# A grouped 3 x 3 convolution on one core: 5 of 8 images combined instead of 3 of 5, and one measurement pass moved ahead of a copy in the ramp

## The chip, the cores and the metric

The kernel runs on one core of a Trainium2 chip. Five engines work side by side: PE multiplies matrices into PSUM banks, DVE (VectorE), ACT (ScalarE) and POOL (GpSimd) do the work per element, SP issues most DMAs. The metric is the device time in microseconds (us); smaller is better. A profiled execution gives a span, from its first to its last instruction, and is timed itself as well.

## The reference

160 images of 128 channels and 32 x 32 pixels are each normalised in 32 groups of 4 channels. Then comes a 3 x 3 convolution with padding 1, 128 channels in and 128 out. Image number 32n + b of the kernel is image b of set n: each of five sets has weights of its own, which are first rounded down to two levels. The input is added to the result.

```python
beta, alpha = max(U), min(U)
s1 = (beta - alpha) / 3.0
v1 = s1 * floor(U / s1)
s2 = s1 / 5.0
v2 = s2 * floor((U - v1) / s2)
w = (v1 + v2).reshape(OUT_CH * N, IN_CH, 3, 3)
xb = gn(x).reshape(B // N, N * C, H, W)          # gn: 32 groups, eps 1e-5
act = conv(xb, w, padding=1, feature_group_count=N)
out = x + act.reshape(B, C, H, W)
```

## The kernel before

**Precision.** A normalised image is split into a high part in fp16 (`hi`, or `vh`) and the fp16 rest (`lo` and its combinations `rows`, or `vl`). Both are multiplied by the integer weights and summed in PSUM.

**Two kinds of images.** Every image has two PSUM banks, `even` and `odd`. Before the main products the even bank gets sums that serve both (`begin` with quarter 2 of the operand, `complete` with quarter 3). Then ACT copies the even bank to `half` (`leave`, L907), and DVE makes the odd bank out of twice `half` minus the even bank (`odd_from_even`, L914). So `complete` comes after the copy `half` and after `begin`, `odd_from_even` after `complete`, and `main(i, 0)`, which writes the even bank again, after `odd_from_even`.

- An *uncombined* image is split as it is. The low part is combined by rows on DVE (`low_part`, `combinations`: L747, L760, L768, L769), and the high part goes through all taps. `begin` and `complete` take 3 matmuls each, the two `main` 12 each: 30.
- A *combined* image is first combined by columns in f32: POOL does the outer columns and a difference (L674, L704), DVE the rest (`combine`: L686, L693). ACT scales it to `vh` (L734), DVE makes `vl` (L740). All four blocks take 6 matmuls: 24.

`combined(i)` decides, by the number alone: none below 7, the odd ones below 30 (`FIFTHS`), i % 5 in {0, 2, 4} below 130 (`THIRDS`), three of four after that.

**Statistics.** ACT reads each image twice, for its sum (L241) and for its squares (L248), unless the image is one of eight in `BY_VECTOR`, which DVE measures. Groups of 8 images from 24 on (of 2 and 4 before) share the small steps: PE averages over channels, DVE, ACT (`ve`), POOL (`rstd`) and DVE make the scale. For an uncombined image `z` is normalised by POOL (L710); for the first image of a group, and the first seven of all, by ACT (L636), which for these also needs DVE's `shift`. A measurement runs up to 16 images ahead.

**Order.** The schedule is written by hand: each engine runs its instructions in the order in which the program names them. The loop over i calls `conv(i, ...)` for PE and hangs the other engines' work for later images around it: in iteration i, from 14 on, DVE makes the low part of image i + 3, ACT the high part of i + 4, POOL and DVE the combination of i + 5. ACT's order in an iteration is: `half`, the first pass of a measurement, the copies of the two banks of image i - 1 to `sum` (L942), the high part, the second pass, now and then a step of the weights (L134, L564).

From `TWO_AHEAD` = 28 on (`steady`), PE does `complete` of i + 1, `begin` of i + 2 and then the two `main` of i, and ACT makes the copy of i + 2 after the first passes. In the ramp before that, PE does `begin` of i + 1, `main(i, 0)`, `complete` of i + 1, `main(i, 1)`, and the copy of i + 1 is named in `conv`, ahead of the passes.

Weights of the next set are quantised in small steps between the images (`Later`), mostly on DVE, with two of each column's steps on ACT. The store of the input (SP) and the adding store of `sum` (POOL, L963) write the result. Loads run 18 images ahead as far as the 11 buffers allow.

Of the kernel before, what the change touches and what calls it, by code (L numbers as in the profile page):

```python
# [36 lines left out]
class Later:  # L37
# [25 lines left out]
    def finish(self):  # L63
        run(self.steps)
# [110 lines left out]
def last_of(steps, last=None):  # L175
    for last in steps:
        pass
    return last


def run(steps):

    while True:
        try:
            next(steps)
        except StopIteration as end:
            return end.value
# [134 lines left out]
def general_path(tc, keep, steps, x, u, out):  # L322
# [8 lines left out]
    with tc.If(far > 0), ExitStack() as ctx:  # L331
# [9 lines left out]
        for n in range(N_SETS):  # L341
            un = one.tile([P, C, TAPS], F32, tag="u", name=f"g_u{n}")
            nc.sync.dma_start(un, uv[n])
            wn = one.tile([P, C, TAPS], F32, tag="w", name=f"g_w{n}")
            k1, k2 = run(steps.quantise(one, un, f"g{n}", F32))
            nc.vector.tensor_scalar_mul(wn, k1, steps.s1)
            nc.vector.scalar_tensor_tensor(wn, k2, steps.s2, wn, ALU.mult, ALU.add)
# [38 lines left out]
class Main:  # L386
# [23 lines left out]

    STAT_LEAD = 15
    FURTHER = 11
    TWO_AHEAD = 28
    LOAD_LEAD = 18
    CHUNKS = 11
    STEADY = 7
# [174 lines left out]
    def keep_sums(self, n, col):  # L591
        wt = self.wts[n, col]
        run(self.both_sums(
            self.nc.gpsimd, wt[:, self.SUM], wt[:, self.DIFF], *(wt[:, k] for k in range(ROW))
        ))
# [51 lines left out]
    def combined(self, i):  # L647

        if i < self.STEADY or i >= self.imgs:
            return False  # L650

        if i < self.FIFTHS:
            return i % 2 == 1
        return i % 5 % 2 == 0 if i < self.THIRDS else i % 4 != 2

    def by_scalar_too(self, i):

# [201 lines left out]
    def steady(self, i):  # L859

        return i >= self.TWO_AHEAD

    def conv(self, i, on_the_way):


        ahead = range(i + 1, self.imgs)[:1]
        if self.steady(i) and self.steady(i - 1):
            for k in ahead:
                self.complete(k)
            for k in range(i + 2, self.imgs)[:1]:  # L870
                self.begin(k)
            self.main(i, 0, lambda: on_the_way(self.COLS[1]))
            self.main(i, 1, lambda: on_the_way(self.COLS[2]))
        elif i == self.FIRST:
            self.main(i, 0)
            self.begin(i + 1)
            on_the_way(self.COLS[1])
            self.main(i, 1)
            on_the_way(self.COLS[2])
            self.leave(i + 1)  # L880
            self.complete(i + 1)
        else:
            self.begin(i + 1)
            self.main(i, 0, lambda: on_the_way(self.COLS[1]))
            self.leave(i + 1)
            self.complete(i + 1)
            if self.steady(i):
                self.begin(i + 2)
            self.main(i, 1, lambda: on_the_way(self.COLS[2]))
        del self.v[i]  # L890
# [102 lines left out]
    def run(self):  # L993
# [54 lines left out]
        def measure(stage, *images):  # L1048
            for i in images:
                self.measure(i, (stage,))  # L1050
# [71 lines left out]
        ready, middle, scaled, measured, loaded = [], [], [], self.EARLY, 6  # L1122
        due = [(c, c) for c in range(1, loaded)]
        later, turned = Later(), []
        for i in range(self.imgs):
# [3 lines left out]
            def on_the_way(col):  # L1129
                if col == self.COLS[1]:  # L1130
                    for st in ready:
                        st.means(self.pg)
                    for *column, parts in self.columns:
                        self.turn_column(*column, parts)
                        turned.append(column)
                    self.columns.clear()
                if col == self.COLS[2]:
                    for st in middle:
                        st.variances()

            if i < self.FIRST:
                if i == self.FIRST - 1:
                    self.begin(self.FIRST)
                    self.leave(self.FIRST)

                j = (i - 1) % self.FIRST
                self.direct_hi(j, self.COLS[2])
                self.direct_lo(j, self.COLS[2])
                if i == self.FIRST - 1:
                    self.complete(self.FIRST)  # L1150
                if i == 0:
                    self.stats[2].variances()
                    self.stats[2].deviation()
                    self.stats[2].power()
                    self.stats[2].scales()
                    run(self.sums_across(0, nc.gpsimd))
                for col in self.COLS:
                    on_the_way(col)
            else:
                j = i - 1  # L1160
                self.conv(i, on_the_way)
            ahead = i + min(10 + i // 3, self.STAT_LEAD + 1)
            to_measure = range(measured, min(self.imgs, ahead))
            measured += len(to_measure)
            if i == 2:
                self.load_set(1)
            if b == self.per_set - 8 and n + 2 < N_SETS:
# [5 lines left out]
                        36 / (self.per_set - 6 - b),  # L1173
                    )
            later.next_image()
            by_scalar = [k for k in to_measure if not self.by_vector(k)]
            by_vector = [k for k in to_measure if self.by_vector(k)]

            if i < self.FIRST:

                if i == 0:
                    measure(0, 8, 9, 10)
                if i == 1:
                    self.normalise(4)
                    self.high_part(4)
                if i == 2:
                    self.normalise(5)
                    measure(1, 9)
                    self.high_part(5)
                    self.odd_from_even(3)  # L1190
                    self.low_part(4)
                    run(self.combinations(4))
                    measure(0, 11)
                self.residual(j)
            else:

                last = None
                for k in self.step_of(i, 2):
                    if self.combined(k):
                        last = last_of(self.low_combined(k), last)  # L1200
                    else:
                        self.low_part(k)
                        later.take(1)
                        last = last_of(self.combinations(k), last)
                last = later.take(1, last)
                if last:
                    before = self.last_but_one(last)
                    for st in scaled:
                        self.after(st.power(), before)
                    for k in self.step_of(i, 4):  # L1210
                        self.beside_pairs(k, before)
                if i > self.FIRST and self.by_hand(j):
                    self.residual(j)
                for k in by_scalar:
                    self.measure(k, (0,))
                if self.steady(i) and i + 2 < self.imgs:
                    self.leave(i + 2)
                if i > self.FIRST and not self.by_hand(j):
                    self.residual(j)
                    self.accumulate(j)  # L1220
                for st in ready:
                    if not st.late:
                        st.deviations()
                for k in self.step_of(i, 3):
                    if self.combined(k):
                        self.high_combined(k)
                        continue
                    if self.by_scalar_too(k):
                        self.normalise(k)
                    self.high_part(k)  # L1230
                for k in by_scalar:
                    self.measure(k, (1,))
# [95 lines left out]
```

## Time and profile before

| | |
|---|---|
| device time, median of 3 runs | 972.56 us |
| lowest and highest | 971.38 and 973.38 us |
| the profiled execution's own time | 971.98 us |
| its span | 970.2 us, granted clock 0.993 |
| PE busy | 928.3 us, 96% |
| ACT busy | 863.3 us, 89% |
| DVE busy | 858.9 us, 89% |
| POOL busy | 446.0 us, 46% |
| DMA | 254.23 MB, mean 262 GB/s |

The profiled execution lies 0.58 us below the median of the runs, and 1.8 us of its time are outside the span. Busy shares are means over the whole span. The stages are: start and weights to about 40 us, the ramp with one image ahead to about 220 us, the steady stretch to about 800 us, then 30 images three of four of which are combined, and the end. In the ramp and in the steady stretch different things can set the pace, so the busy times are read by stage.

### The profile page before, as it was taken

Reading aid. Unit: us, or ns where it says so; the run is one execution under the profiler, and the core shown is the slowest. Engines: PE = TensorE matmul, PEld = TensorE weight load, DVE = VectorE, ACT = ScalarE, POOL = GpSimd, SP = SyncE. Lnnn points to the kernel's source line nnn. Section 1 sums busy time; section 2 is a strip of 40 time slices with the busy share of each in tenths; the row PEclk is TensorE's granted clock in tenths of the full one; section 3 lists DMA queues with packets and bytes.
Section 4 is the critical chain, followed back from the end, with each engine's and each line's share of the span. In section 5 each row is a group of like instructions: output and inputs, shape, how many; then the busy total and the mean of one; then the engine's idle time right before and its main releaser. Section 6 shows DMA issues by size and latency. Waiting matters only on the chain.

```text
span 970.2 us, 12948 instructions
## 1 busy us (share of the span) xinstructions
PE 928.3 (96%) x4432; PEld 434.6 (45%) x4432; DVE 858.9 (89%) x1125; ACT 863.3 (89%) x1320; POOL 446.0 (46%) x481
## 2 busy tenths in 40 slices
PE   2899979999999999999999999999999999999996
PEld 1444434444444444444444444444444444444442
DVE  7988878888899899998999899898989988889973
ACT  5779879998999999999999999999999999997660
POOL 4354433544453443454445444545444455454640
PEclk9999989999999999999999999999999999999998
DMA  9079999999999999999999999999999999756554
GB/s 353 29 270 351 329 353 330 328 326 329 321 314 317 259 283 294 276 284 269 290 252 308 286 282 284 289 277 297 263 274 266 290 280 258 162 90 102 95 93 128
DMA packets 67450, 254.23 MB, mean 262 GB/s; under 512 B 5296, under 2 KB 5296, under 8 KB 67376
## 3 DMA queue, kind: packets, MB, share of 16 engines
q1 hardware_dynamic: 45344, 173.09, 47.8%
q0 software_dynamic: 22032, 80.23, 44.1%
q8 instruction: 37, 0.61, 0.2%
q14 instruction: 37, 0.30, 0.1%
HBM read 89.19 MB, written 164.10 MB: 261 GB/s over the span
## 4 chain that ended last, share of the span: by engine, by line
PE 79%; ACT 10%; DVE 5%; issue 3%; DMA 2%; POOL 1%; SPq 0%; DVEq 0%; ACTq 0%; POOLq 0%
PE even L839 43%; PE odd L839 14%; PE even L784 11%; PE odd L784 11%; ACT junk L248 2%; ACT vh L734 2%; ACT sum L942 2%; ACT junk L241 2%; DMA u<-in_L_conv_U_dram 2%; ACT z L636 1%; ACT half L907 1%; ACT hi L644 1%; DVE ext L508 1%; DVE ext L509 1%; DVE lo L747 1%
## 5 line engine op out<-in xcount | busy, mean ns | idle before, releaser
L839 PEld LDWEIGHTS <-wt 128*128 128x128 f16 x1884 | 184.3, 99 | 211.2 <-issue 4.4
L740 DVE SCALAR_TENSOR_TENSOR vl<-v,rstd,vh 128x2048 f16<-128x2048 f32 x94 | 235.2, 2502 | 48.6 <-ACT vh L734 48.4
L839 PE MATMUL even<-vh,across 128*128 128x512 f16 x564 | 211.3, 375 | 3.5 <-ACT half L907 3.5
L839 PE MATMUL even<-vl,across 128*128 128x512 f16 x564 | 211.3, 375 | 1.7 <-DVE vl L740 1.7
L734 ACT ACTIVATE vh<-v,rstd 128x2048 f16<-128x2048 f32 x94 | 190.2, 2024 | 0.0
L784 PEld LDWEIGHTS <-wt 128*128 128x128 f16 x1242 | 121.7, 100 | 144.2 <-issue 6.6
L248 ACT ACTIVATE junk<-xt,mv 128x1024 uint8<-128x1024 f32 x152 | 176.4, 1160 | 0.3
L839 PE MATMUL even<-rows,wt 128*128 128x512 f16 x567 | 174.2, 381 | 2.5 <-ACT half L907 2.4
L963 POOL DMA_DIRECT2D out_dram<-sum x153 | 135.2, 884 | 89.7 <-ACT sum L942 74.5
L241 ACT ACTIVATE junk<-xt 128x1024 uint8<-128x1024 f32 x152 | 161.2, 1060 | 12.7 <-DMA xt<-in_x_dram 9.8
L839 PEld LDWEIGHTS <-across 128*128 128x128 f16 x1128 | 110.4, 98 | 135.5 <-issue 7.5
L784 PE MATMUL even<-hi,wt 128*128 128x496 f16 (+3 forms) x594 | 162.9, 379 | 4.8 <-DVE odd L914 3.8
L710 POOL TENSOR_SCALAR z<-xt,ngm,rstd 128x1024 f32<-128x1024 f32 x49 | 91.8, 1873 | 152.1 <-DVE rows L769 50.5
L784 PE MATMUL odd<-hi,wt 128*128 128x496 f16 (+3 forms) x594 | 161.0, 375 | 0.0
L686 DVE TENSOR_TENSOR v<-xt 128x960 f32<-128x960 f32 x94 | 155.8, 1658 | 0.5 <-POOL v L674 0.5
L907 ACT COPY half<-even 128x512 f32<-128x512 f32 x157 | 90.6, 577 | 60.1 <-PE even L839 57.1
L674 POOL TENSOR_SCALAR v<-xt,ngm 128x64 f32<-128x64 f32 x94 | 59.0, 628 | 172.8 <-DVE vl L740 74.8
L914 DVE SCALAR_TENSOR_TENSOR odd<-half,even 128x512 f32<-128x512 f32 x157 | 107.8, 687 | 17.3 <-PE even L839 13.8
L839 PE MATMUL even<-vh,wt 128*128 128x496 f16 (+1 forms) x282 | 105.6, 375 | 0.0
L839 PE MATMUL even<-vl,wt 128*128 128x496 f16 (+1 forms) x282 | 105.6, 375 | 0.0
L839 PE MATMUL odd<-vl,wt 128*128 128x496 f16 (+1 forms) x282 | 105.6, 374 | 0.0
L839 PE MATMUL odd<-vh,wt 128*128 128x496 f16 (+1 forms) x282 | 105.6, 374 | 0.0
(148 smaller groups left out, 1131.1 us busy)
## 6 DMA issues: line engine op xcount, KB each, us to landing
xt<-in_x_dram SPq DMA_DIRECT2D x78, 1024.0 KB, 9.6
out_dram<-sum POOLq DMA_DIRECT2D x153, 512.0 KB, 8.8
out_dram<-xt SPq DMA_DIRECT2D x76, 1024.0 KB, 14.2
out_dram<-xt SPq DMA_DIRECT2D x7, 512.0 KB, 6.1
u<-in_L_conv_U_dram SPq DMA_DIRECT2D x4, 576.0 KB, 14.7
xt<-in_x_dram SPq DMA_DIRECT2D x4, 512.0 KB, 9.8
range<-in_L_conv_U_dram SPq DMA_DIRECT2D x3, 576.0 KB, 8.0
u<-in_L_conv_U_dram SPq DMA_DIRECT2D x2, 288.0 KB, 3.0
```

The lines of the kernel that those rows point to most:

```text
L241: self.nc.scalar.activation(junk, image, ACTF.Copy, scale=-1.0 / image.shape[1], accum_out=self.mv[:, j, 0:1],)
L248: self.nc.scalar.activation(junk, image, ACTF.Square, bias=self.mv[:, j, 0:1], accum_out=self.mv[:, j, 1:2],)
L674: return self.nc.gpsimd.tensor_scalar(self.view(self.v[i], 0, (512 + W // 2 - 1, 2), (W // 2, H)), self.view(self.image(i), 1, (W - 3, 2), ...
L686: nc.vector.tensor_tensor(self.view(v, 1, (511, 2), (half, H), (1, half - 1)), self.view(x, 1, (1, 2), (W, H), (2, half - 1)), self.view(x ...
L710: ins = nc.gpsimd.tensor_scalar(z, self.image(i), st.ngm[:, j], st.rstd[:, j], ALU.add, ALU.mult)
L734: self.nc.scalar.mul(vh, self.v[i], st.rstd[:, j])
L740: yield self.nc.vector.scalar_tensor_tensor(vl, self.v[i], st.rstd[:, j], self.hi[i], ALU.mult, ALU.subtract)
L784: nc.tensor.matmul(target[a][:, first:end, c0:c1], self.wts[n, col][:, k, :], tile[:, s0 : s0 + 2 * (end - first) - 1 : 2, c0 + dw : c1 + dw],
L839: self.nc.tensor.matmul(out, weights, moving, start=start and j == 0, stop=False, skip_group_check=True)
L907: self.nc.scalar.copy(half, self.eo[i][0])
L914: self.nc.vector.scalar_tensor_tensor(odd, self.half.pop(i), 2.0, even, ALU.mult, ALU.subtract)
L963: added = self.nc.gpsimd.dma_start(self.ov[n, :, b], self.sum.pop(i), accum_op=ALU.add)
```

## The change

Three edits. `combined` takes, between 30 and 130, the images with i * 5 % 8 < 5, that is i % 8 in {0, 2, 4, 5, 7}. `TWO_AHEAD` becomes 20. And for i from 4 to 19 the first pass of the first image that ACT measures in this iteration is named inside `conv`, between `main(i, 0)` and `leave(i + 1)`; to have it there, the list of images to measure is made before `conv` instead of after it. Where an iteration measures a second image on ACT, its first pass stays behind the copy.

```diff
-    TWO_AHEAD = 28
+    TWO_AHEAD = 20
...
         if i < self.FIFTHS:
             return i % 2 == 1
-        return i % 5 % 2 == 0 if i < self.THIRDS else i % 4 != 2
+        return i * 5 % 8 < 5 if i < self.THIRDS else i % 4 != 2
...
-    def conv(self, i, on_the_way):
+    def conv(self, i, on_the_way, between):
...
             self.begin(i + 1)
             self.main(i, 0, lambda: on_the_way(self.COLS[1]))
+            between()
             self.leave(i + 1)
             self.complete(i + 1)
             if self.steady(i):
...
+            ahead = i + min(10 + i // 3, self.STAT_LEAD + 1)
+            to_measure = range(measured, min(self.imgs, ahead))
+            measured += len(to_measure)
+            by_scalar = [k for k in to_measure if not self.by_vector(k)]
+            by_vector = [k for k in to_measure if self.by_vector(k)]
+            first_of = by_scalar[:1] if self.FIRST < i < self.TWO_AHEAD else []
...
                 j = i - 1
-                self.conv(i, on_the_way)
-            ahead = i + min(10 + i // 3, self.STAT_LEAD + 1)
-            to_measure = range(measured, min(self.imgs, ahead))
-            measured += len(to_measure)
+                self.conv(i, on_the_way, lambda: measure(0, *first_of))
...
-            by_scalar = [k for k in to_measure if not self.by_vector(k)]
-            by_vector = [k for k in to_measure if self.by_vector(k)]
-
...
-                for k in by_scalar:
+                for k in by_scalar[len(first_of):]:
                     self.measure(k, (0,))
```

## The prediction

> **What bounds the kernel now.** I read the page first (busy shares, the row of slices), then the busy time by stage, then the timelines of PE, ACT and DVE in the stages where PE is not full.
>
> ```profile
> span 970.2 us, 12948 instructions
> PE 928.3 (96%) x4432; PEld 434.6 (45%) x4432; DVE 858.9 (89%) x1125; ACT 863.3 (89%) x1320; POOL 446.0 (46%) x481
> ...
> PE   2899979999999999999999999999999999999996
> ...
> 100.00:160.00 60.00, 52.40 (x242) 24.07 (x241) 51.91 (x83) 51.21 (x80) 19.37 (x22) 0.94 1.04 343
> ...
> 137.00:142.00 5.00, 5.00 (x13) 1.87 (x13) 2.81 (x2) 2.19 (x3) 3.52 (x5) 0.52 1.03 419
> ...
> 160.00:240.00 80.00, 79.31 (x384) 37.33 (x383) 68.73 (x97) 73.73 (x118) 40.24 (x44) 1.00 1.04 327
> 240.00:520.00 280.00, 280.00 (x1345) 131.31 (x1343) 258.46 (x321) 272.49 (x422) 129.60 (x132) 1.00 1.02 288
> 520.00:800.00 280.00, 280.00 (x1349) 131.56 (x1347) 255.94 (x329) 271.98 (x417) 135.04 (x135) 1.00 1.00 282
> 800.00:880.00 80.00, 78.35 (x373) 36.41 (x372) 69.77 (x70) 76.15 (x116) 40.40 (x40) 1.00 0.77 164
> ```
>
> The stage rows give stretch, length, busy us of PE, PEld, DVE, ACT, POOL, granted clock, DMA share, GB/s. From 240 to 800 (images 33 to 129) PE has no idle time at all; ACT is 97% busy, DVE 92%. There, work taken off PE shortens the run as long as ACT (7.5 and 8.0 us idle in the two rows) keeps up. The ramp loses PE time at 100 to 160, and the clock drops there.
>
> ```profile
> 117.55 0.38 PE L839 MATMUL even<-vh,across 128*128 128x512 f16 x1
> ...
> 118.82 0.80 PE L784 MATMUL even<-hi,wt 128*128 128x512 f16 x3
> ...
> 122.95 0.80 PE L784 MATMUL odd<-hi,wt 128*128 128x512 f16 x3
> ...
> 125.50 0.81 PE L839 MATMUL even<-rows,wt 128*128 128x512 f16 x3
> 126.15 0.38 PE L839 MATMUL even<-vh,wt 128*128 128x512 f16 x1
> ...
> 137.00 1.41 PE L784 MATMUL even<-hi,wt 128*128 128x512 f16 x3 [2.79 <-DVE odd L914]
> ...
> 171.74 0.81 PE L839 MATMUL even<-rows,wt 128*128 128x512 f16 x3 [0.69 <-ACT half L907]
> ```
>
> ```profile
> 90.29 0.81 PE L839 MATMUL even<-rows,wt 128*128 128x512 f16 x3 [0.45 <-ACT half L907]
> ```
>
> ```profile
> 89.68 0.56 ACT L907 COPY half<-even 128x512 f32<-128x512 f32 x1
> ...
> 100.83 0.59 ACT L907 COPY half<-even 128x512 f32<-128x512 f32 x1 [2.54 <-PE even L839]
> ...
> 820.57 0.57 ACT L907 COPY half<-even 128x512 f32<-128x512 f32 x1
> ...
> 826.27 0.57 ACT L907 COPY half<-even 128x512 f32<-128x512 f32 x1
> ...
> 831.57 0.59 ACT L907 COPY half<-even 128x512 f32<-128x512 f32 x1 [0.45 <-PE even L839]
> ```
>
> ```profile
> 128.37 0.16 DVE L296 TENSOR_SCALAR twice<-small 128x4 f32<-128x4 f32 x1 [1.26 <-ACT wt L564]
> ```
>
> Columns: start, length, engine, line, operation; in brackets the idle time before it and what ended it. Images are counted by the program's order. PE waits for `half` (the copy of the even bank) at 90.29 and 171.74, ACT waits for PE at 100.83, DVE waits at 128.37 for ACT's `wt`, PE at 137.00 for DVE's `odd`.
>
> **The change, part by part.**
>
> (1) *5 of 8 instead of 3 of 5.* Counting 30 to 129: before 60 combined images, after 62 (60 in 32..127, then 31 and 128). A combined image is four blocks of 6 matmuls, each 1.27 us (117.55 to 118.82): 5.08. An uncombined one is two blocks of 3 at 0.65 (125.50 to 126.15) and two of 12 at 2.55 (122.95 to 125.50): 6.40. Two images at 1.32: **-2.6 us of PE**, where PE is the bound.
>
> The Trainium skill ("TensorE: Matmul & The Clock Gate", "Wait — 56ns, not 53.3ns?") gives a warm matmul N / 2.4 GHz plus about 2.5 ns. By that the blocks of 12 are 2.50 and of 3 0.63, an uncombined image 6.26, and two images would bring 2.4. The row says that matmuls with 16 x 31 strided columns don't get the shorter time; I take 2.6.
>
> On the other engines: ACT, two `vh` (2.02) for two `hi` (1.06), +1.9. All group starts from 32 on become combined, where before five (48, 56, 88, 96, 128) were not and had their `z` on ACT: -5 x 1.25 = -6.3. ACT -4.4 in all. DVE: (2.50+1.66+0.74) for (1.22+0.69+0.42+0.42) twice, +4.3, less five `shift`: hidden in DVE's 8% idle (21 us per 280). POOL +9.0 (two more of 0.63+1.08, three more `z` of 1.87) at 47% busy. DMAs keep number and order on both queues. If this cover were gone, the +4.3 of DVE alone would eat the gain.
>
> (2) *Evenness of the pattern.* Between two `half` copies ACT takes 5.70 if the image normalised there is combined (820.57 to 826.27 in its timeline), 4.8 if not (826.27 to 831.57 less 0.45 to 0.54 of wait: idle 0.45, and the pass before it ends in a short read of its sum). PE's stretch is complete(i+1), begin(i+2), main(i). The new order C N C N C C N C has four combined of five. Lead of the copy at place 6: at most what one combined main leaves, 2.54-0.6 = 1.9 (trace 1.75 to 1.9). The next stretch is 0.65+1.27+2.54 = 4.46 against ACT's 5.70: lead at place 7 is **0.65**. The old order never goes below 1.6 by the same working, but its `z` took 1.25 off: around images 47 to 49 and 87 to 89 its leads are 0.05 to 0.2, and PE still shows no gap. The new order has no `z`. Places 129, 130 (two uncombined) bring the lead to about 0.1 once. Quantising steps (0.6 to 0.9) can fall before place 7; I allow **+0.3** in all, with 0 and +3 as ends (12 times 0.25).
>
> (3) *The first pass ahead of the copy, i = 4 to 19.* In 13 iterations (copies 6 to 8, 10 to 19) a pass of 1.06 stands before `half`. Behind it on ACT wait that copy, then both `sum` copies; for the copy wait PE's complete and DVE's `odd`. Where ACT was waiting for PE (copies 10 and 16: 2.54, 6.92) the pass is free; elsewhere the copy is 1.06 later. The pass reads a chunk issued 20 us or more before (65.16 for the pass at 101.31; median landing 9.6): no new DMA wait.
> Followed through: copy 6 had a lead of 0.44, PE loses 0.6; copy 8 had none, PE is now 1.06 late in all (90.29 becomes 91.35). From then on PE is late itself, and copies up to 14 find it so: the delays don't add. At copy 10 ACT spends 1.06 of its wait on the pass, but starts 1.06 later; `wt` at 127.86 therefore stands where it stood. DVE's chain from 128.37 hangs on it, and PE's restart at 137.00 on that chain's `odd`. **So the 1.06 is swallowed there: 0.** Were `wt` 1.06 earlier, -1.06; were PE's lateness kept, +1.06: these are the ends.
> From 146.55 ACT is a pass ahead, and copy 20 has no pass before it (image 34 is measured by DVE): it comes 1.06 earlier, and the stall of 0.69 goes: **-0.7**. Next in line is DVE's `odd` of 20, 1.7 ahead of its use.
>
> The clock: PE's gaps around 130 are 1.28, 1.70 and 2.79, none over 2.8, yet the granted clock is 0.52 over 137 to 142: 13 matmuls in 5.0 us, about 2.3 lost. The same page ("What's actually happening") puts the half rate after an idle window of about 3.4 us; by it gaps like these cost nothing, and mine after (1.3, 0.6, 2.8) would be free too: 2.3 less. The trace says that a bunch of shorter gaps is enough, and I take the loss as kept: 0, ends -2.3 and +2.3.
>
> (4) *Two ahead from 20 instead of 28.* No instruction added; `begin` of images 22 to 29 comes one image earlier. So far their low parts end 6.3 to 9.5 us ahead of it; one image takes off 5.7, so 0.6 to 3.8 stay, and ACT, free of its waits, brings them earlier. PE has no gap at 172 to 240, so the four ACT waits it removes (0.44, 0.74, 1.20, 0.28) bring nothing: 0. If the leads were gone, eight waits of up to 1 us.
>
> Sum against the profiled execution: 971.98 (span 970.2) -2.6 +0.3 -0.7 = 969.0. The median of the runs is 0.58 above that execution: **969.5**.
>
> **Rivals.**
> *ACT becomes the bound in the new runs.* For: 97% busy, lead 0.65. If each of 12 cycles costs 0.25, 3.0 goes back in place of 0.3: 972.2, no change. Against: ACT's sum falls by 4.4.
> *Slower: the late copies starve PE in the ramp.* If each delay is paid in full beyond its lead (copies 6: 0.62, 8: 1.01, 11: 1.01, 12: 0.78, 14: 1.01, 17: 0.86, 18: 1.01, 19: 0.65), 7.0: 972.56-2.6-0.7+7.0 = 976.3. It decides once the ramp loses over 3.3 us (2.6 + 0.7), for slower by over 0.2% once it loses 5.2. Against: the lateness is shared, and 137.00 hangs on DVE.
> *The ramp gains.* `wt` earlier and the clock kept: -1 to -3 more, 967.5.
> *The change hardly does what it says*: 60 to 62 images is little, and if the 2.6 were offset nothing but the 0.7 would be left: 971.9; it goes with no change.
>
> **How the numbers follow.** This kernel's measurement tells about 0.2% (1.9 us) from no change: faster means below 970.6, slower above 974.5. Sum as worked out: 0.59. Ramp gains: 0.12. ACT bound or nothing left: 0.14. Ramp starved: 0.15. Faster 0.71, same 0.14, slower 0.15. The likeliest case alone spans 968.3 to 970.5. For 8 in 10 the range takes the ramp gain down to 966.8 and the no-change cases up to 972.8, leaving out the starved ramp and the far end of the gains.
>
> **What would show it.** Right: PE busy without gap from about 172 to 800, that stretch 2.6 shorter; 12 fewer matmuls; 12 `z` on ACT instead of 17; at 90 a gap of about 1 before complete(8); no gap at complete(20); the restart of main(14) again at about 137. Wrong: PE gaps ended by `half` once per eight images after 240; PE still late by 1 us or more at 146; gaps in 172 to 240 ended by `vl` or `rows`.

## The result, and the profile after

| | before | after |
|---|---|---|
| device time, median of 5 runs each, side by side | 971.38 us | 967.40 us |
| lowest and highest | 970.93 and 973.38 | 966.99 and 968.49 |
| ratio, with its 95% interval | | 0.9954 (0.9940 to 0.9968) |
| the profiled execution's own time and span | 971.98, 970.2 us | 968.49, 966.7 us |

The changed kernel is 4.0 us faster in the medians (0.41%), and 0.46% by the ratio, which would be 4.5 us. 969.5 was predicted, from a median of 972.56: a difference of 3.1 us. The profiled execution of the changed kernel is the slowest of its five.

First the page of the changed kernel, then its busy time by stage (stretch, length, busy us of PE, PEld, DVE, ACT, POOL, granted clock, DMA share, GB/s):

```profile
span 966.7 us, 12926 instructions
...
PE 926.6 (96%) x4420; PEld 433.7 (45%) x4420; DVE 866.8 (90%) x1118; ACT 860.8 (89%) x1315; POOL 447.3 (46%) x488
...
PE   2899989999999999999999999999999999999996
```

```profile
40.00:60.00 20.00, 19.16 (x90) 8.89 (x89) 15.68 (x35) 14.77 (x24) 10.26 (x20) 0.91 0.25 88
...
100.00:160.00 60.00, 53.39 (x244) 24.38 (x242) 51.81 (x84) 50.74 (x80) 19.19 (x22) 0.94 1.04 344
160.00:240.00 80.00, 80.00 (x388) 37.66 (x387) 70.15 (x98) 75.53 (x118) 43.42 (x45) 1.00 1.05 324
240.00:520.00 280.00, 280.00 (x1346) 131.48 (x1345) 262.62 (x322) 271.35 (x420) 131.05 (x135) 1.00 1.01 290
520.00:800.00 280.00, 280.00 (x1349) 131.65 (x1348) 261.80 (x324) 270.90 (x418) 136.33 (x138) 1.00 1.01 284
800.00:880.00 80.00, 78.33 (x373) 36.39 (x372) 71.67 (x71) 76.06 (x115) 35.77 (x41) 1.00 0.76 156
```

4420 matmuls instead of 4432. From 160 to 800 PE is full: the idle 0.7 us of the row 160 to 240 is gone, and the two long rows are full as before, although DVE has 4.2 and 5.9 us more to do there (258.46 and 255.94 before). ACT has 1.1 us less in each.

The PE timeline of the ramp, at the places that the prediction followed (start, length, engine, line, operation; in brackets the idle time before it and what ended it):

```profile
91.48 0.81 PE L839 MATMUL even<-rows,wt 128*128 128x512 f16 x3 [0.75 <-ACT half L908]
...
130.09 0.81 PE L839 MATMUL even<-rows,wt 128*128 128x512 f16 x3 [1.33 <-ACT half L908]
...
133.19 0.38 PE L839 MATMUL even<-vl,across 128*128 128x512 f16 x1 [0.66 <-DVE vl L740]
...
137.19 1.41 PE L784 MATMUL even<-hi,wt 128*128 128x512 f16 x3 [2.80 <-DVE odd L915]
...
171.61 0.81 PE L839 MATMUL even<-rows,wt 128*128 128x512 f16 x3
```

complete(8) comes at 91.48 instead of 90.29, the restart of main(14, 0) at 137.19 instead of 137.00, and complete(20) has no gap in front of it. What the restart hangs on stands nearly where it stood, in the timelines of ACT and DVE:

```profile
128.06 0.47 ACT L564 ACTIVATE wt<-small 128x384 f16<-128x384 f32 x1
128.44 1.04 ACT L241 ACTIVATE junk<-xt 128x1024 uint8<-128x1024 f32 x1
129.38 0.19 ACT L241 ACTIVATION_READ_ACCUMULATOR junk<-xt 128x1 f32 x1
129.47 0.57 ACT L908 COPY half<-even 128x512 f32<-128x512 f32 x1
```

```profile
128.56 0.16 DVE L296 TENSOR_SCALAR twice<-small 128x4 f32<-128x4 f32 x1 [1.14 <-ACT wt L564]
```

The second line of ACT is the moved pass, now ahead of the copy; `wt` is at 128.06. In the timeline of the kernel before it is

```profile
127.86 0.47 ACT L564 ACTIVATE wt<-small 128x384 f16<-128x384 f32 x1
```

**A ledger by image.** In each trace take the end of the last matmul into the odd bank of an image, less the same end in the trace before. A minus means earlier than before, in us. The columns that matter: at image 0 nothing of the change has acted; from 18 to 31 lies complete(20); from 31 to 129 lies the steady stretch with the new pattern.

| end of odd of image | 0 | 6 | 10 | 14 | 18 | 31 | 129 | 159 | 31 to 129 |
|---|---|---|---|---|---|---|---|---|---|
| after | +0.88 | +0.89 | +1.19 | +0.60 | +0.73 | -0.14 | -3.00 | -2.97 | -2.86 |
| pattern alone | +0.02 | +0.02 | -0.23 | -0.91 | -0.91 | -0.93 | -3.78 | -3.73 | -2.85 |
| two ahead alone | +1.05 | +1.05 | +0.81 | +1.09 | +1.09 | +1.08 | +1.06 | +1.06 | -0.02 |
| pass alone | -0.02 | +0.81 | +1.25 | -0.42 | -0.28 | -1.13 | -1.18 | -1.14 | -0.05 |
| all, two passes only | +0.14 | +0.14 | -1.04 | -0.89 | -0.89 | -1.34 | -4.20 | -4.17 | -2.86 |

Of the 3.5 us between the two spans 2.97 stand at the last matmul; the rest lies behind it (8.3 us from there to the end before, 7.3 to 7.9 in the five kernels of the table), where nothing was changed, and why it differs is not known.

### The profile page after: what moved, and what is told of

Read it like the earlier page. It is cut to its first block, busy times and chain, and to the rows that moved or that the text cites. A ratio compares the mean times of both kernels' runs of the same rounds, so it can differ in the third digit from the quotient of the medians.

```text
span 966.7 us, 12926 instructions
## 1 busy us (share of the span) xinstructions
PE 926.6 (96%) x4420; PEld 433.7 (45%) x4420; DVE 866.8 (90%) x1118; ACT 860.8 (89%) x1315; POOL 447.3 (46%) x488
## 4 chain that ended last, share of the span: by engine, by line
PE 84%; ACT 8%; DVE 4%; issue 2%; POOL 1%; DMA 0%; DVEq 0%; ACTq 0%
PE even L839 45%; PE odd L839 15%; PE even L784 12%; PE odd L784 11%; ACT vh L734 2%; ACT junk L248 2%; ACT sum L943 1%; ACT junk L241 1%; ACT z L636 1%; DVE ext L508 1%; DVE ext L509 1%; ACT half L908 0%; ACT hi L644 0%; DVE lo L747 0%; DVE tt L144 0%
## 5 line engine op out<-in xcount | busy, mean ns | idle before, releaser
L740 DVE SCALAR_TENSOR_TENSOR vl<-v,rstd,vh 128x2048 f16<-128x2048 f32 x96 | 239.2, 2491 | 37.2 <-ACT vh L734 37.1
L839 PE MATMUL even<-vh,across 128*128 128x496 f16 (+1 forms) x576 | 216.1, 375 | 3.5 <-ACT half L908 3.5
L839 PE MATMUL even<-vl,across 128*128 128x496 f16 (+1 forms) x576 | 215.8, 375 | 0.7 <-DVE vl L740 0.7
L734 ACT ACTIVATE vh<-v,rstd 128x2048 f16<-128x2048 f32 x96 | 194.1, 2022 | 0.0
L839 PE MATMUL even<-rows,wt 128*128 128x512 f16 x549 | 168.6, 381 | 2.2 <-ACT half L908 2.1
L686 DVE TENSOR_TENSOR v<-xt 128x960 f32<-128x960 f32 x96 | 163.3, 1702 | 0.0
L784 PE MATMUL even<-hi,wt 128*128 128x496 f16 (+3 forms) x576 | 158.5, 380 | 4.6 <-DVE odd L915 3.8
L710 POOL TENSOR_SCALAR z<-xt,ngm,rstd 128x1024 f32<-128x1024 f32 x52 | 86.3, 1660 | 160.7 <-DVE vl L740 75.3
L784 PE MATMUL odd<-hi,wt 128*128 128x496 f16 (+3 forms) x576 | 156.8, 376 | 0.0
L674 POOL TENSOR_SCALAR v<-xt,ngm 128x64 f32<-128x64 f32 x96 | 66.3, 691 | 160.8 <-DVE vl L740 86.3
```

What stands on the lines that cost most here:

```text
L674: return self.nc.gpsimd.tensor_scalar(self.view(self.v[i], 0, (512 + W // 2 - 1, 2), (W // 2, H)), self.view(self.image(i), 1, (W - 3, 2), ...
L686: nc.vector.tensor_tensor(self.view(v, 1, (511, 2), (half, H), (1, half - 1)), self.view(x, 1, (1, 2), (W, H), (2, half - 1)), self.view(x ...
L710: ins = nc.gpsimd.tensor_scalar(z, self.image(i), st.ngm[:, j], st.rstd[:, j], ALU.add, ALU.mult)
L734: self.nc.scalar.mul(vh, self.v[i], st.rstd[:, j])
L740: yield self.nc.vector.scalar_tensor_tensor(vl, self.v[i], st.rstd[:, j], self.hi[i], ALU.mult, ALU.subtract)
L784: nc.tensor.matmul(target[a][:, first:end, c0:c1], self.wts[n, col][:, k, :], tile[:, s0 : s0 + 2 * (end - first) - 1 : 2, c0 + dw : c1 + dw],
```

## The experiments

Each ran beside the kernel before on the same chip; ratios are to that.

**Pattern alone.**

```diff
-        return i % 5 % 2 == 0 if i < self.THIRDS else i % 4 != 2
+        return i * 5 % 8 < 5 if i < self.THIRDS else i % 4 != 2
```

> Only the 5 of 8 pattern is taken over; the order in the ramp and the 28 stay. Theory (PE is the bound from 240 to 800 and pays by the matmul): 12 matmuls fewer give 2.6 us, and the five group starts without z on ACT give some tenths more where the copy of the even bank had no lead left; so 2.6 to 3.0 us less than before, PE without idle time from 240 to 800, and the ramp as before (PE waits of 1.28, 1.70, 2.79 at 128 to 137, 0.69 at copy 20). Rival (ACT is the bound, and the gain comes from the five z that left it): up to 6 us less.

968.73 us, ratio 0.9968 (0.9956 to 0.9980), 3.1 us less. In the ledger 2.85 come between images 31 and 129. The 0.91 up to image 14 is not the pattern's, which starts at 30: in that execution the clock was at half rate for 3.4 us at 134 to 143 instead of 6.8 (granted clock 0.81 there, 0.62 before; the reading stands under the pass alone).

**Two ahead from 20, alone.**

```diff
-    TWO_AHEAD = 28
+    TWO_AHEAD = 20
```

> Only the start of working two ahead is moved from 28 to 20; pattern and pass order stay. Theory: PE has no idle time in 172 to 240 but for 0.69 before copy 20, so nothing to win: within 0.7 us of before, and ACT's four waits of 0.28 to 1.20 there shrink. Rival (the low parts of images 22 to 29 come too late one image earlier): PE waits ended by vl or rows, 1 to 4 us slower.

972.22 us, ratio 1.0000 (0.9991 to 1.0008). The ledger is flat from 14 to 159; the 1.05 stands there from image 0 on (the clock at 40 to 44, last section). This edit is worth nothing by itself, though ACT's waits for PE at the copies fall from 6.0 to 4.1 us between 172 and 240.

**The pass alone**, in i = 4 to 19, with the old pattern and TWO_AHEAD at 28:

```diff
+            first_of = by_scalar[:1] if self.FIRST < i < 20 else []
...
-                self.conv(i, on_the_way)
+                self.conv(i, on_the_way, lambda: measure(0, *first_of))
```

> Only the pass is moved ahead of the copy, for i from 4 to 19; pattern and 28 stay. Theory: PE is up to 1 us late after copy 8, that is swallowed where main of image 14 waits for DVE's odd (at about 137 as before), and the 0.69 before copy 20 goes: 0.5 to 0.8 us less than before. Rival (each late copy is paid in full): 7 us more than before.

970.18 us (20 runs), ratio 0.9983 (0.9976 to 0.9990): 1.7 us less, more than the 0.5 to 0.8 expected. The PE timeline shows the steps as worked out:

```profile
77.59 0.81 PE L839 MATMUL even<-rows,wt 128*128 128x512 f16 x3 [0.66 <-ACT half L908]
...
91.54 0.81 PE L839 MATMUL even<-rows,wt 128*128 128x512 f16 x3 [0.89 <-ACT half L908]
...
137.23 0.80 PE L784 MATMUL even<-hi,wt 128*128 128x512 f16 x3 [2.80 <-DVE odd L915]
...
170.60 0.81 PE L839 MATMUL even<-rows,wt 128*128 128x512 f16 x3
```

Copy 6 costs 0.66, copy 8 brings the lateness to 1.25, the restart at 137.23 swallows all but 0.23, and complete(20) has no gap (-0.85 from 18 to 31). What had not been expected is the drop from +1.25 to -0.42 across image 14. It is the clock, in the busy time of two stretches of this kernel:

```profile
134.00:143.00 9.00, 6.20 (x23) 2.43 (x21) 6.05 (x9) 6.09 (x12) 5.24 (x6) 0.81 1.04 409
137.00:142.00 5.00, 4.77 (x15) 1.89 (x15) 3.05 (x3) 3.34 (x5) 3.52 (x5) 0.66 1.03 422
```

and of the changed kernel:

```profile
134.00:143.00 9.00, 6.20 (x17) 2.26 (x16) 6.01 (x9) 6.06 (x12) 5.27 (x6) 0.62 1.04 411
137.00:142.00 5.00, 4.80 (x12) 1.77 (x12) 3.01 (x3) 3.34 (x5) 3.52 (x5) 0.50 1.02 419
```

PE is busy for the same 6.20 of 9 us, but 23 matmuls against 17: 0.81 over 9 us is 3.4 us at half rate, 0.62 is 6.8.

**A pass ahead in two iterations only.** The changed kernel with

```diff
-            first_of = by_scalar[:1] if self.FIRST < i < self.TWO_AHEAD else []
+            first_of = by_scalar[:1] if i in (9, 15) else []
```

so that no copy of a short lead is delayed, and the pass still goes into ACT's waits at copies 10 and 16.

> The changed kernel, but with the pass ahead of the copy only at i = 9 and 15, where ACT waits for PE anyway (2.54 and 6.92 us). Theory (DVE's chain before main of image 14 hangs on ACT's wt, and the passes at i = 5 to 7 made PE late, so that wt gained nothing): copy 8 is in time as before, wt comes 1.06 us earlier, and so main of image 14: 1 us less than the changed kernel, 4.5 us less than before. Rival (that restart hangs on DVE's own queue, or on the clock, not on wt): the same as the changed kernel within 0.3 us.

966.74 us, ratio 0.9946 (0.9932 to 0.9959). Its timelines of ACT, DVE and PE:

```profile
126.79 0.47 ACT L564 ACTIVATE wt<-small 128x384 f16<-128x384 f32 x1
```

```profile
127.29 0.16 DVE L296 TENSOR_SCALAR twice<-small 128x4 f32<-128x4 f32 x1 [1.21 <-ACT wt L564]
```

```profile
135.93 1.41 PE L784 MATMUL even<-hi,wt 128*128 128x512 f16 x3 [2.80 <-DVE odd L915]
```

`wt` is 1.07 us earlier than before the change, and so are `twice` (1.08) and the restart (1.07). PE is itself 1.04 ahead from image 10 on here, so this kernel alone doesn't tell which of the two sets the restart. The others do: in the changed kernel and with the pass alone PE was over 1.2 behind at image 13, and the restart stood within 0.23 of where it was, as `wt` did (128.06 and 128.10). So ACT's lateness, not PE's, sets it, by way of DVE: from `twice` on DVE works without a gap until the `odd` of image 14, 7.9 us later in every one of these traces. The last matmul here ends 1.2 us ahead of the changed kernel's, but 0.74 of that is there at image 0; in the ratios the two intervals overlap, so this version has the lowest median of all that ran and is not shown to be better.

**More combined images.** Is PE still the only limit at 62? The changed kernel with 69 combined images from 30 to 129, and the one with two passes with 65:

```diff
-        return i * 5 % 8 < 5 if i < self.THIRDS else i % 4 != 2
+        return i * 11 % 16 < 11 if i < self.THIRDS else i % 4 != 2
```

> The changed kernel with 11 of 16 images combined between 30 and 130 (69 instead of 62, none of them lost to a group start). PE's work falls by 7 x 1.32 = 9.2 us. ACT's per 16 images is 11 x 5.70 + 5 x 4.76 and its share of the weights, about 89.8 us, against about 89.2 for PE. If PE alone sets the pace at 62: 958.2, 9.2 below the changed kernel. If ACT becomes the bound at that dose (the rival of the prediction, one step further): between 966 and 969, and PE's gaps in the steady stretch are ended by half, in all some 7 to 10 us.

968.13 us, ratio 0.9953 (0.9939 to 0.9966): 9.2 us of PE's work less than the changed kernel, and the same time. Its busy time by stage, and its costliest groups of PE from 240 to 800 (after the bar: busy us, mean ns, idle us before them and what ended it):

```profile
240.00:520.00 280.00, 275.31 (x1316) 128.47 (x1315) 268.19 (x314) 273.69 (x420) 135.29 (x139) 1.00 1.01 292
520.00:800.00 280.00, 277.33 (x1332) 129.79 (x1330) 268.80 (x324) 274.05 (x419) 141.98 (x141) 1.00 1.01 283
```

```profile
L839 PE MATMUL even<-vh,across 128*128 128x496 f16 (+1 forms) x405 | 151.7, 375 | 4.8 <-ACT half L908 4.7
L839 PE MATMUL even<-vl,across 128*128 128x496 f16 (+1 forms) x405 | 151.7, 374 | 2.2 <-DVE vl L740 2.2
```

7.4 us of PE's idle time came back, two thirds of it ended by `half` and the rest by `vl`. Added up from start to start of the matmuls, with what a matmul of the same shape takes subtracted, the stalls come to 10.4 us, more than the 9.2 saved: from image 18 to 129 the changed kernel gains 3.73 in the ledger, this one 2.72. So the rival of the prediction, ACT as the bound, is true one step further for the larger part. At the three stalls of `vl` DVE had waited 0.97 for POOL's `rstd` just before; how far ACT stands behind that is not settled.

```diff
-        return i * 5 % 8 < 5 if i < self.THIRDS else i % 4 != 2
+        return i * 21 % 32 < 21 if i < self.THIRDS else i % 4 != 2
```

> Two passes ahead (e4_two_passes) with 21 of 32 images combined between 30 and 130: 65 instead of 62, PE 4.0 us less. If ACT still keeps up at this dose: 962.7, 4.0 below e4_two_passes. If ACT holds it already: 965.5 to 967, with short PE gaps ended by half. Three of the group starts (56, 88, 120) are uncombined here and have their z on ACT, 1.25 each, which makes stalls at the copies behind them likely.

967.97 us, ratio 0.9952 (0.9939 to 0.9966), 1.0 us above the range expected if ACT holds it. Three stalls of 0.7 stand behind the three uncombined group starts:

```profile
378.18 0.38 PE L839 MATMUL even<-vh,across 128*128 128x512 f16 x1 [0.69 <-ACT half L908]
```

The same count of stalls gives 4.8 us, again more than the 4.0 saved: 2.6 at these three, the rest in nine of 0.2 to 0.3. From image 18 to 129 the kernel with 62 and two passes gains 3.31, this one 2.55. Of the doses tried, 62 of 100 is the highest that pays. An order with 65 in which every group start is combined was not tried; by this count it would keep some of the 4.0.

**Taking work off ACT.** The same two doses, with six more images measured by DVE instead of ACT, and passes ahead at 9 and 15 only:

```diff
-    BY_VECTOR = (8, 10, 11, 14, 19, 24, 29, 34)
+    BY_VECTOR = (8, 10, 11, 14, 19, 24, 29, 34, 45, 61, 77, 93, 109, 125)
```

> Two passes ahead (e4_two_passes), 69 images combined between 30 and 130 (as e5_eleven_of_16), and six more images (45, 61, ... 125) measured by DVE: each takes 2.3 us off ACT and puts 1.9 on DVE (two L231 of 0.68, one aggregate of 0.21, two of 0.15). If ACT alone took back the 9.2 us in e5_eleven_of_16, half or more of the 7 us of stalls in the steady stretch go, and the time is 961 to 964. If DVE is as near its limit (268 of 280 us busy in that kernel, and three of its stalls ended by vl), the stalls turn to vl and the time stays at 966 to 968.

971.22 us (13 runs), ratio 0.9994 (0.9986 to 1.0003): neither theory's number; worse than both, and than the 0.9953 of 69 images with ACT measuring. Busy time by stage and a group of PE:

```profile
240.00:520.00 280.00, 274.31 (x1312) 128.09 (x1311) 271.93 (x331) 266.38 (x404) 136.25 (x137) 1.00 1.02 291
520.00:800.00 280.00, 275.40 (x1321) 128.82 (x1320) 270.55 (x336) 267.16 (x405) 143.95 (x142) 1.00 1.01 280
```

```profile
L839 PE MATMUL even<-vl,across 128*128 128x496 f16 (+1 forms) x403 | 150.9, 374 | 9.7 <-DVE vl L740 9.7
```

ACT is relieved by 7 us in each row, and of its stalls in that stretch none but the one of 0.3 at image 130 is left. DVE takes their place at 97%: 9.7 us of PE's waits are now for `vl`. One of them, in the timelines of DVE and PE:

```profile
330.16 1.27 DVE L231 BATCH_NORM_STATS2 st<-xt 128x6 f32<-128x512 f32 x2
...
331.84 2.34 DVE L740 SCALAR_TENSOR_TENSOR vl<-v,rstd,vh 128x2048 f16<-128x2048 f32 x1
```

```profile
334.24 0.38 PE L839 MATMUL even<-vl,across 128*128 128x512 f16 x1 [0.73 <-DVE vl L740]
```

The measurement stands right ahead of the `vl` that PE waits for.

> The same six images measured by DVE, with 65 images combined (as e9_21_of_32), so that DVE has more room. ACT's relief is 2.3 us per 16 images against 1.3 x 3 of PE's work over the whole stretch. If ACT was the bound there: 963 to 965, 2 to 4 below e9_21_of_32, with the stalls at copies 57, 89 and 121 gone. If the z of the uncombined group starts alone makes those stalls: they stay, and the time is 966 to 967.5.

969.63 us (11 runs), ratio 0.9979 (0.9970 to 0.9988): also slower than with ACT measuring. The stalls at 57, 89 and 121 shrank from about 0.7 to 0.43 to 0.46, and new ones came:

```profile
340.77 0.38 PE L839 MATMUL even<-vl,across 128*128 128x512 f16 x1 [0.75 <-DVE vl L740]
...
378.65 0.38 PE L839 MATMUL even<-vh,across 128*128 128x512 f16 x1 [0.43 <-ACT half L908]
```

So at 65 and at 69 combined images moving these six measurements to DVE costs time: the 14 to 15 us that DVE is idle in 280 at 65 (264.85 and 266.01 busy) are no cover for a burst of 1.7 us ahead of a `vl`. Other places for the measurements, and the move at 62, were not tried.

**Later weights.** Is the work on the second set's weights what holds the ramp at 128 to 137? The changed kernel with the quantising begun at image 9:

```diff
-                if b == (4 if n == 0 else 1):
+                if b == (9 if n == 0 else 1):
```

> The changed kernel with the quantising of the second set's weights begun at image 9 instead of 4. If the chain through ACT's wt and DVE's twice is what holds main(14,0) at 137, the steps leave the ramp, the gaps of PE between 125 and 140 shrink from 6.6 us to 2 or less, the clock stays full there (2.3 to 3.4 more), and the time falls by 3 to 7 us against the changed kernel. If the ramp is held by the supply of images (loads, measurements, scales) and the weights only happen to stand there, the gaps stay and the time moves by less than 1 us; if the steps squeezed into fewer images come late for image 32, PE stalls there and the time rises by 2 or more.

967.73 us, ratio 0.9953 (0.9939 to 0.9967): as the changed kernel. The PE timeline, and the stretch around the restart:

```profile
91.49 0.81 PE L839 MATMUL even<-rows,wt 128*128 128x512 f16 x3 [1.64 <-ACT half L908]
...
111.52 0.38 PE L839 MATMUL even<-vh,across 128*128 128x512 f16 x1 [2.37 <-ACT half L908]
...
131.62 0.81 PE L839 MATMUL even<-rows,wt 128*128 128x512 f16 x3 [0.79 <-ACT half L908]
...
137.85 0.79 PE L784 MATMUL even<-hi,wt 128*128 128x512 f16 x3 [2.74 <-DVE odd L915]
```

```profile
134.00:143.00 9.00, 6.26 (x31) 2.78 (x29) 8.45 (x12) 7.61 (x14) 4.15 (x5) 1.00 1.03 388
```

One part of the theory came: in this execution the clock stays full (31 matmuls in these 9 us instead of 17), and PE goes from 2.77 behind at image 13 to 1.48 ahead at 14. But the wait of 2.74 for `odd` is still there, and the stalls at copies 8 and 11 grew to 1.64 and 2.37 (0.75 and 1.83 in the changed kernel), which eats the gain. The theory that the weights alone hold the ramp falls. The timeline of DVE says what holds the restart here:

```profile
129.17 0.15 DVE L296 TENSOR_SCALAR twice<-small 128x4 f32<-128x4 f32 x1
...
137.10 0.69 DVE L915 SCALAR_TENSOR_TENSOR odd<-half,even 128x512 f32<-128x512 f32 x1
```

`twice` doesn't wait any more, but DVE is busy without a gap from 126.5 on, and `odd` comes 7.9 us behind `twice` as before. With `wt` out of the chain, DVE's own work is next.

> The same late quantising, with a pass ahead of the copy only in iterations 9 and 15. In e4_two_passes this brought 0.6 us in the median (1.2 in the profiled executions), since ACT reached wt 1.06 earlier. If wt is no longer in the chain, passes at 6 to 8 cost what they cost PE (0.7 to 1.1 at copy 8), so this kernel is again 0.5 to 1 below e7_late_quant; if late quantising changes nothing, it equals e4_two_passes.

The same with passes at 9 and 15 only: 967.16 us, ratio 0.9943 (0.9930 to 0.9957), which can't be told from two passes without it. It is 2.0 ahead at image 14, but complete(20) waits 0.94 for its copy again, where the kernel with two passes and early weights waits 0.26.

## Why the prediction was right

The prediction said 3.1 us less; the medians say 4.0. The time itself came out 2.1 lower than predicted, 1.2 of which is the kernel before, at 971.38 in this comparison instead of 972.56. The terms summed to -3.0; in the ledger of the profiled executions the changed kernel gains 3.70 from image 18 to the end (+0.73 to -2.97). Terms 1 and 3 below make up that difference. What the medians and the ratio have above 3.7 is not accounted for; the clock (5) is the likely place, which is not shown. By its steps:

1. *Pattern, -2.6, with +0.3 for its evenness.* The 12 matmuls went, ACT's `z` fell to 12 as worked out, and the stretch from image 31 to 129 gave 2.85 or 2.86 in all five kernels with 62 combined images. The allowance is the term that was mis-sized, with the wrong sign: the new order has no stall at place 7 (ACT's smallest lead, from the end of a copy to the start of its `complete`, up to image 129 is 0.55, at image 39 and eleven more; where PE waits it is 0.05), while the *old* order had two of about 0.15 behind uncombined group starts, at complete(49) and complete(89), too short to stand in the brackets. The ledger of the changed kernel steps by -0.15 at both; they went together with the `z` of those starts. Where two uncombined images follow each other, at 129 and 130, 0.11 is given back. 2.64 + 0.30 - 0.11 = 2.83 of the 2.86; with the rule's 2.4 in place of the trace's 2.64 it would be 2.59. The sums for the other engines were off where it cost nothing: over the span DVE has 7.9 us more to do instead of at most 4.3 (its L686 takes 1.70 each instead of 1.66; why is not shown), ACT 2.5 less instead of 4.4, POOL 1.3 more instead of 9.0.

2. *The pass ahead of the copies.* Copy 6 and copy 8 did what was worked out (0.66; 1.25 late in all) in the kernel with the pass alone. In the changed kernel's execution copy 6 lost nothing: a wait for a load was missing on ACT, and 0.30 were added at copy 8. That its complete(8) came at 91.48, near the 91.35 worked out, is therefore luck: 0.88 of its lateness was there at image 0, from the clock. The restart swallowed the lateness in both, to within 0.23 (the +0.60 at image 14 of the changed kernel is 0.19 there and the rest behind it, in matmuls at the low clock), since ACT's `wt` stood still; with two passes `wt` came 1.07 earlier and the restart too, which was the named end of -1.06.

3. *complete(20), -0.7.* -0.87 in the ledger; -0.85 with the pass alone, 0 without it. A bracket counts the idle time past a matmul's modelled end; measured from start to start a stall is about 0.15 longer than its bracket (0.84 for the 0.69 at copy 57 with 65 combined images), and that is what is gained.

4. *Two ahead, 0.* 0, in the run for it alone.

5. *The clock, 0 between -2.3 and +2.3.* The profiled execution kept the loss (0.50 over 137 to 142), as said. But this is not one number: over 65 runs of the kernel before, 38 had a mean clock of 0.992 and a median of 972.37; the other 27 had 0.994 to 0.997 and medians of 970.3 to 971.1. Of the 20 runs with the pass alone 16 had 0.995 or more. So part of the 1.7 us that this edit brought may be a clock that loses less in more of the runs, which one trace of each can't show. That the smaller gap at 133 (0.66 instead of 1.70) makes this so is argued, not shown: with two passes that gap is 1.70 again, and four runs of five had 0.994.

The rivals: the ramp did not starve, for the reason given. ACT did not become the bound at 62, and did, for the larger part of the stalls, at 65 and 69; the lead of 0.55 at place 7 was all there was.

## What to carry to other kernels

Where one engine is full over a stretch, work taken off it is worth its time in the trace, to about a tenth here, until the next engine's lead at the tightest place of the cycle is used up: work out that lead, not the mean share, to find the last dose that pays. A delay on a path with waits need not add up; follow it to the next place where another chain restarts the engine, and ask on what that chain hangs. Try the edits one at a time: here the sum of pattern (3.1) and pass (1.7) was the whole, to within the intervals, and the third edit was nothing.

## What the hardware showed that was not expected

In the traces here the half rate of PE's clock came in whole lengths of 3.4 us: 0, 3.4 or 6.8 us of it lay in the same 9 us (1.00, 0.81 and 0.62 in the rows above). The idle time there doesn't tell which: with the pass alone and in the changed kernel PE was busy for 6.20 of these 9 us and for 4.03 and 4.01 of the 6 us before them, with 3.4 and 6.8 us of half rate. (With late weights, at 1.00, PE had been busy for 5.21 of those 6 us.) The half rate also comes where the program was not changed at all: the changed kernel's profiled execution had the clock at 0.57 over 40 to 44, the kernel before at 1.00.

```profile
40.00:44.00 4.00, 4.00 (x12) 1.46 (x11) 3.72 (x7) 3.97 (x6) 2.11 (x4) 0.57 0.01 4
```

```profile
40.00:44.00 4.00, 3.98 (x19) 1.88 (x20) 3.72 (x7) 3.97 (x5) 2.24 (x4) 1.00 0.01 4
```

The first row is of the changed kernel, the second of the one before. Of the twelve traces three have such a stretch (0.57 to 0.60 there), and in these PE is 0.88 to 1.05 us late at image 0; in the other nine it is within 0.16 of before.

The Trainium skill ("TensorE: Matmul & The Clock Gate", "What's actually happening") has the activity measured in windows of about 3.4 us that run on regardless of the program; the lengths here agree with that. Its half rate after an idle window doesn't: no gap of PE around 130 was longer than 2.8 us, and the clock fell all the same. For forecasts of a fraction of a per cent this is a spread of one to two microseconds that no reading of one trace takes away.
